# Softmax denominators of two neighbouring key tiles by one product with ones: an adaLN block with attention and experts on one core

## The chip, the core and the metric

The kernel runs on one core of a Trainium2 chip. Its engines are named as in the profile: PE (TensorE, products), DVE (VectorE), ACT (ScalarE), POOL (GpSimd) and SP (SyncE, which issues DMAs); each runs its own instructions in its own order, and semaphores order them against each other. The metric is the time of one execution on the device, in microseconds (us).

## What is computed

One transformer block over 4 batches of 2048 tokens with 256 channels, in fp32. Cut to what matters:

```python
h = layernorm(x) * (1 + ca) + sa              # per batch
q, k, v = split(h @ w_qkv)                    # 8 heads of 32
scores = q @ k.T * scale                      # causal
scores = scores + head_scales * (q[:3] . dirs) * (k[:3] . dirs)
x = x + ga * (softmax(scores) @ v) @ w_out
h = layernorm(x) * (1 + cb) + sb
shared = sum over 2 experts of gelu(h @ up) @ down
routed = the 4 most probable of 16 experts, each weighted by its probability
x = x + gb * (shared + routed)
```

What the change is about is the softmax: for each query, the exponentials of its scores are multiplied with the values, and divided by their own sum over all keys.

## The kernel before

The 8192 tokens are 16 blocks of 512 queries (`QB`); four blocks make a batch, and `qb = i % 4` is a block's place in it. A block attends to `4 * (qb + 1)` tiles of 128 keys (`kb`), for two quads `g` of four heads each. So block i has `ks = 8 * (qb + 1)` steps `(g, kb)`, numbered n, and the kernel has 320; in 224 of them all 512 queries are used, in the others (the diagonal) 384, 256 or 128.

A block has two stages. In the first (`fill_in`, called at line 1450 with steps of `project_steps`, `dense_steps`, `tile_steps` and `out_steps`) PE makes the projections of a coming block, the output projection of the block before, the shared experts and the tiles of routed experts. In the second, the summing stage (line 1456 to the end of the loop), it runs the attention of block i. The maxima of the scores of block i + 1 (`max_steps`, products `ps`, then DVE's mask and maximum) are spread over both stages.

A step of the summing stage (`sum_steps`, line 665) has three parts:

- `probabilities(kb)`, line 679: four products `st` (keys by queries, one for each head of the quad, each in a 32-row strip of PE) into two PSUM tiles of two heads each, four small products that take off the maxima, and on the diagonal four for the mask; then ACT makes two exponentials of 128x1024 (line 713) into the two halves of one SBUF tile `pt`, of which there are two (`probs`, `bufs=2`).
- `weigh(kb, 0)`, line 718: the product `av` of the probabilities with the values, added up in PSUM over all kb.
- `weigh(kb, 1)`: the product `dv` of the probabilities with `ones`, added up in another PSUM bank: the sums by which the result is divided.

The PSUM tiles of the scores come from a ring of three pairs (`mring`, line 149), which the maxima use too; the sums from `accp`, two banks. After the last kb, DVE copies the sums into `rd` (line 736), ACT copies the products into `num` (line 739), and `divide` (line 741) makes a reciprocal and a product for each of four parts, into `oT`.

The order is written out by hand. Everything of a summing stage goes into the list `part` with a key, and `run` calls it by rising key (equal keys in the order in which they were put in); each engine keeps the order in which its instructions were made (`Pinned`, line 41: hence all instructions have line 52 in the profile). Scores have key n, `av` n + 1.3, `dv` n + 1.6:

```python
        for n, (first, average, total) in enumerate(sums + more):
            part.append((n, first))
            part.append((n + 1.3, average))
            part.append((n + 1.6, total))
```

So PE's order in a step is st(n), av(n-1), dv(n-1). The products of a search for maxima have key at + 0.5, in `searched` steps (line 1486). DVE's work (divisions, the choice of experts, the two layer norms) is spread by `put` (line 1489), which books each piece with its cost in us against the `room` of a step, 2.2 us or 1.4 in a searched step, and gives it the key at + 0.6. The `ticks` (line 1524) pace POOL's gathers and scatters of routed rows at n + 0.9; the combination of gathered rows (`combine`, `complete`, line 1217, DVE's `sum`) runs with them when their rows are asked for, outside `room`. SP loads the inputs, the weights of the experts and the rows; `load_gates` has the gates of a batch made.

Of the kernel before, what the change touches and what calls it, by code (L numbers as in the profile page):

```python
# [12 lines left out]
F32 = mybir.dt.float32  # L13
# [6 lines left out]
P = 128  # L20
# [72 lines left out]
def adaln_block_kernel(  # L93
# [178 lines left out]
        for k in range(TOPK):  # L272
            nc.vector.memset(nth[:, t, k : k + 1], float(TOPK * t + k + 1))
    tile_no = const.tile([P, MAXT], F32, tag="tile_no", name="tile_no")
    tile_no_i = const.tile([P, MAXT], I32, tag="tile_no_i", name="tile_no_i")
    nc.gpsimd.iota(tile_no_i, pattern=[[1, MAXT]], base=0, channel_multiplier=0)
    nc.vector.tensor_copy(tile_no, tile_no_i)
    half_power = const.tile([P, TT], F32, tag="half_power", name="half_power")
# [139 lines left out]
    def max_steps(i, g):  # L418

        qb = i % NB  # L420
        parts = small.tile([P, TT, 4, NB], F32, tag="parts", name=f"parts{i}_{g}")
        mTs[i, g] = work.tile([P, QB], BF16, tag=f"mT{g}", name=f"mT{i}_{g}")
        steps = []

        def scores(t, ch):
            w = min(QB, (qb * TT + t + 1) * P - ch * QB)
            halves = []
            for a in range(2):
                both = pair(f"ps{i}_{g}_{t}_{ch}_{a}")
                halves.append(both)  # L430
                for u in range(2):
                    r = G * (2 * a + u)
                    nc.tensor.matmul(
                        both[:, u, :w],
                        lhsT=qTs[i][r : r + G, g, t * P : (t + 1) * P],
                        rhs=kT[r : r + G, (i - qb + ch) % SLOTS, g, :w],
                        start=True,
                        stop=True,
                        tile_position=(r, 0),
                    )  # L440
            for a, both in enumerate(halves):
                if ch == qb:
                    edge = both[:, :, w - P : w]
                    nc.vector.tensor_tensor(edge, edge, c_pair, ALU.add)
                nc.vector.tensor_reduce(
                    parts[:, t, 2 * a : 2 * a + 2, ch], both[:, :, :w], AX.X, ALU.max
                )

        def split():
            pc = pieces[g]  # L450
            ngm = small.tile([P, TT, 4], F32, tag="ngm", name=f"ngm{i}_{g}")
            nc.vector.tensor_reduce(ngm, parts[:, :, :, : qb + 1], AX.X, ALU.max, negate=True)
            for n in range(3):
                nc.vector.tensor_copy(pc[:, :, :, n], ngm)
                if n < 2:
                    nc.vector.tensor_tensor(ngm, ngm, pc[:, :, :, n], ALU.subtract)

        def turn():
            pc = pieces[g]
            pr = single([P, QB], f"pr{i}_{g}")  # L460
            for t in range(TT):
                nc.tensor.matmul(
                    pr[:, t * P : (t + 1) * P],
                    lhsT=pc[:, t].rearrange("p h n -> p (h n)"),
                    rhs=ident_b,
                    start=True,
                    stop=True,
                )
            nc.scalar.copy(mTs[i, g], pr)

        for t in range(TT):
            for ch in range(qb + 1):
                steps.append(lambda t=t, ch=ch: scores(t, ch))
        return steps, split, turn
# [183 lines left out]
        left = fill_in(merged(project_steps(2), gates_to_come[4:]), tops[:10])  # L658
        rest = tops[10:]

    probs = ctx.enter_context(tc.tile_pool(name="probs", bufs=2))
    tiles = ctx.enter_context(tc.tile_pool(name="tiles", bufs=2))
    kept = ctx.enter_context(tc.tile_pool(name="kept", bufs=3))

    def sum_steps(i, g, oT):

        qb = i % NB
        nkb = (qb + 1) * TT
        qT, mT = qTs[i], mTs[i, g]
        sums = []  # L670
        pts, held = {}, {}

        def keys(kb):
            return (i - qb + kb // TT) % SLOTS, kb % TT

        def left(kb):
            return max(0, kb - qb * TT) * P

        def probabilities(kb):
            lo = left(kb)  # L680
            slot, n = keys(kb)
            halves = [pair(f"st{i}_{g}_{kb}_{a}") for a in range(2)]
            heads = [both[:, u, :] for both in halves for u in range(2)]
            for h in range(4):
                r = G * h
                nc.tensor.matmul(
                    heads[h][:, lo:],
                    lhsT=kT[r : r + G, slot, g, n * P : (n + 1) * P],
                    rhs=qT[r : r + G, g, lo:],
                    start=True,  # L690
                    stop=False,
                    tile_position=(r, 0),
                )
            for h in range(4):
                r = G * h
                nc.tensor.matmul(
                    heads[h][:, lo:],
                    lhsT=unit3[r : r + 3, :],
                    rhs=mT[r : r + 3, lo:],
                    start=False,  # L700
                    stop=(kb < qb * TT),
                    tile_position=(r, 0),
                )
            if kb >= qb * TT:
                for h in range(4):
                    nc.tensor.matmul(
                        heads[h][:, lo : lo + P],
                        lhsT=ident_b,
                        rhs=kmask,
                        start=False,  # L710
                        stop=True,
                    )
            pt = probs.tile([P, 4, QB], F32, tag="pt", name=f"p{i}_{g}_{kb}")
            for a, both in enumerate(halves):
                nc.scalar.activation(pt[:, 2 * a : 2 * a + 2, lo:], both[:, :, lo:], AF.Exp)
            pts[kb] = pt

        def weigh(kb, s):
            if kb == 0:
                sums.append(accp.tile([P, QB], F32, tag="acc", name=f"{'ad'[s]}v{i}_{g}"))  # L720
            lo = left(kb)
            slot, n = keys(kb)
            for h in range(4):
                r = G * h
                c0 = g * P + r
                nc.tensor.matmul(
                    sums[s][r : r + G, lo:],
                    lhsT=ones if s else vA[:, slot, n, c0 : c0 + G],
                    rhs=pts[kb][:, h, lo:],
                    start=(kb == 0),  # L730
                    stop=(kb == nkb - 1),
                    tile_position=(0, r),
                )
            if kb == nkb - 1 and s:
                held["rd"] = once.tile([P, QB], F32, tag="rd", name=f"rd{i}_{g}")
                nc.vector.tensor_copy(held["rd"], sums[1])
            elif kb == nkb - 1:
                held["num"] = once.tile([P, QB], F32, tag="num", name=f"num{i}_{g}")
                nc.scalar.copy(held["num"], sums[0])

        def divide(t):
            own = slice(t * P, (t + 1) * P)
            rd = held["rd"]
            nc.vector.reciprocal(rd[:, own], rd[:, own])
            nc.vector.tensor_tensor(oT[:, g, own], held["num"][:, own], rd[:, own], ALU.mult)

        steps = [
            [
                lambda kb=kb: probabilities(kb),
                lambda kb=kb: weigh(kb, 0),  # L750
                lambda kb=kb: weigh(kb, 1),
            ]
            for kb in range(nkb)
        ]
        return steps, [lambda t=t: divide(t) for t in range(TT)]

    def out_steps(i, oT):

# [66 lines left out]
    def turn_steps(i):  # L825
# [14 lines left out]
        def logits():  # L840
            pl = single([P, TT, R], f"pl{i}")
            for t in range(TT):
                for k in range(KC):
# [4 lines left out]
                        start=(k == 0),  # L848
                        stop=(k == KC - 1),
                    )  # L850
            logs[i] = small.tile([P, TT, R], F32, tag="log", name=f"log{i}")
            nc.scalar.copy(logs[i], pl)

        return [(T_US, lambda: turn(0)), (T_US, lambda: turn(1)), (2.2, logits)]
# [1 line left out]
    def choice_steps(i, group):  # L856
# [39 lines left out]
        def chosen():  # L896
# [3 lines left out]
            held["sel"] = sel  # L900
            if group is None:

                gate = small.tile([P, TT, R], F32, bufs=1, tag="gate", name=f"gate{i}")
                parts = small.tile([P, TT, 3, R], BF16, bufs=1, tag="gate3", name=f"gate3_{i}")
                nc.vector.tensor_tensor(gate, pr[:, :, :R], sel, ALU.mult)
                for n in range(3):
# [52 lines left out]

        def weights():  # L960
            t0 = group.blocks.index(i) * TT
            wide = once.tile(shape, F32, tag="hotp", name=f"hotp{i}")
            pr = held["pr"]
            nc.vector.tensor_tensor(
                wide, hot(), pr[:, :, :R].unsqueeze(2).broadcast_to(shape), ALU.mult
# [438 lines left out]
    for i in range(NBLK):  # L1404
# [58 lines left out]
        if i == 0:  # L1463
            load_gates(0)
        oT = once.tile([P, KC, QB], F32, tag="oT", name=f"oT{i}")
        (sums, divided), (more, ends) = [sum_steps(i, g, oT) for g in range(NQ)]
        part = []
        for n, (first, average, total) in enumerate(sums + more):
            part.append((n, first))
            part.append((n + 1.3, average))  # L1470
            part.append((n + 1.6, total))
        for n, (_, ss, turn) in enumerate(rest):
            at = int(0.93 * (n + 0.5) / len(rest) * ks)
            part += [(at + 0.5, s) for s in ss]
# [45 lines left out]
        for n, j in enumerate(fresh):  # L1520
            till = 0.95 if n + 1 == len(fresh) else 0.5
            put(norm(first_norm_steps(j)), (0.15 + 0.4 * n) * ks, till * ks)

        def ticks(n):
            tick()
# [100 lines left out]
```

## Time and profile before

| | us |
|---|---|
| median of 3 runs | 2571.34 |
| the runs | 2566.7, 2571.34, 2572.5 |
| profiled execution, its own time | 2561.29 |
| profiled execution, span of the trace | 2559.6 |
| mean granted clock of TensorE in it | 0.955 of full |

| groups of the profiled execution | us busy | mean ns of one |
|---|---|---|
| PE st, 512 queries (x1792) | 324.1 | 651 |
| PE av, 512 queries (x1792) | 244.2 | 617 |
| PE dv, 512 queries (x1792) | 240.8 | 610 |
| ACT exponential 128x1024 (x448) | 434.2 | 1021 |
| DVE maximum of ps 128x1024 (x448) | 529.9 | 1221 |
| POOL gathers of rows (x224) | 216.7 | 968 |

Busy time is the time in which at least one instruction of the group ran; four strips of PE run side by side, so eight records of `dv`, one step, cover 1.075 us and not 8 x 0.61. The column "idle before" of such a group is time in which its engine had nothing to run just before an instruction of the group, and the name behind the arrow is who let it go on. A line of the timeline gives the start in us, the length, the engine, and the operation with the tiles that it writes and reads.

### The profile page before, as it was taken

Reading aid. Unit: us, or ns where it says so; the run is one execution under the profiler, and the core shown is the slowest. Engines: PE = TensorE matmul, PEld = TensorE weight load, DVE = VectorE, ACT = ScalarE, POOL = GpSimd, SP = SyncE. Lnnn points to the kernel's source line nnn. Section 1 sums busy time; section 2 is a strip of 40 time slices with the busy share of each in tenths; the row PEclk is TensorE's granted clock in tenths of the full one; section 3 lists DMA queues with packets and bytes.
Section 4 is the critical chain, followed back from the end, with each engine's and each line's share of the span. In section 5 each row is a group of like instructions: output and inputs, shape, how many; then the busy total and the mean of one; then the engine's idle time right before and its main releaser. Section 6 shows DMA issues by size and latency. Waiting matters only on the chain. (4 is left out here: it accounts for less than half of the span.)

```text
span 2559.6 us, 42608 instructions
## 1 busy us (share of the span) xinstructions
PE 2397.4 (94%) x16961; PEld 1182.3 (46%) x16961; DVE 1427.1 (56%) x2833; ACT 981.4 (38%) x1391; POOL 698.0 (27%) x740
## 2 busy tenths in 40 slices
PE   7989999999999999999999999998999998998987
PEld 4443433345544333365645344364633257335754
DVE  5577665436667774346565656458557840422235
ACT  2324244543333344534343335533342343542420
POOL 3201010421124035201013333502353320354334
PEclk9989899999999899998999999998998999999999
DMA  2300403343532112233622135233623169338943
GB/s 87 118 1 9 148 9 109 115 132 116 163 114 67 34 44 99 73 115 122 211 95 75 50 126 179 82 129 112 221 90 109 56 200 300 110 121 278 325 136 116
DMA packets 219703, 306.91 MB, mean 120 GB/s; under 512 B 18544, under 2 KB 158832, under 8 KB 219504
## 3 DMA queue, kind: packets, MB, share of 16 engines
q1 hardware_dynamic: 192720, 228.89, 27.1%
q0 software_dynamic: 25536, 73.43, 9.0%
q8 instruction: 134, 2.20, 0.4%
q10 hardware_dynamic: 1248, 1.86, 0.2%
q14 instruction: 65, 0.53, 0.1%
HBM read 193.49 MB, written 114.82 MB: 120 GB/s over the span
## 5 line engine op out<-in xcount | busy, mean ns | idle before, releaser
L52 DVE TENSOR_REDUCE parts<-ps 128x2 f32<-128x1024 f32 (+3 forms) x640 | 662.4, 1063 | 318.4 <-PE ps L52 309.3
L52 ACT ACTIVATE p<-st 128x1024 f32<-128x1024 f32 (+3 forms) x640 | 538.6, 893 | 618.8 <-PE st L52 564.4
L52 PE MATMUL st<-qT,kv 32*128 32x512 f32 (+3 forms) x2560 | 412.0, 584 | 15.2 <-ACT p L52 7.6
L52 PE MATMUL ps<-kv,qT 32*128 32x512 f32 (+3 forms) x2560 | 400.8, 614 | 22.1 <-DVE parts L52 11.9
L52 POOL DMA_INDIRECT got<-yg,at x224 | 216.7, 968 | 368.5 <-ACT p L52 96.9
L52 PE MATMUL av<-p,kv 128*32 128x512 f32 (+3 forms) x2560 | 306.6, 549 | 3.8 <-ACT p L52 2.1
L52 PE MATMUL dv<-p,ones 128*32 128x512 f32 (+3 forms) x2560 | 302.3, 541 | 1.5 <-issue 1.5
L72 POOL DMA_INDIRECT xg<-rows,at x219 | 212.8, 972 | 299.5 <-ACT p L52 121.2
L52 PEld LDWEIGHTS st<-qT,kv 32*128 32x128 f32 x2560 | 143.9, 186 | 268.9 <-issue 196.2
L52 DVE TENSOR_TENSOR ps<-ps,cmask 128x256 f32<-128x256 f32 x256 | 109.3, 427 | 253.1 <-PE ps L52 208.6
L52 PEld LDWEIGHTS ps<-kv,qT 32*128 32x128 f32 x2560 | 135.0, 194 | 229.5 <-issue 90.2
L52 POOL TENSOR_TENSOR x<-x,tmps 128x512 f32<-128x512 f32 x28 | 35.4, 1264 | 519.8 <-DVE tmps L52 519.7
L52 PE MATMUL pu<-xt,wt 128*128 128x128 f32 x1216 | 161.3, 283 | 13.9 <-DMA wt<-experts 12.2
L52 PE MATMUL py<-wt,tact 128*128 128x256 f32 x608 | 163.6, 403 | 7.6 <-ACT xt L52 2.1
L52 PEld LDWEIGHTS pu<-xt,wt 128*128 128x128 f32 x1216 | 151.4, 195 | 37.1 <-issue 12.9
L52 PE MATMUL st<-mT,unit 3*128 3x512 bf16 (+3 forms) x1280 | 165.9, 348 | 0.0
L52 PEld LDWEIGHTS dv<-p,ones 128*32 128x32 f32 x2560 | 72.4, 110 | 174.0 <-issue 168.7
L52 ACT COPY y<-py 128x512 f32<-128x512 f32 x152 | 89.0, 585 | 144.1 <-PE py L52 141.5
L52 PEld LDWEIGHTS py<-wt,tact 128*128 128x128 f32 x608 | 111.1, 196 | 50.3 <-issue 9.0
L52 DVE RECIPROCAL rd<-rd 128x128 f32<-128x128 f32 x128 | 120.8, 943 | 0.8
L52 ACT COPY xt<-px 128x512 f32<-128x512 f32 x152 | 86.3, 586 | 85.2 <-PE px L52 82.1
L52 PEld LDWEIGHTS av<-p,kv 128*32 128x32 f32 x2560 | 52.6, 108 | 137.4 <-issue 112.4
(288 smaller groups left out, 2454.0 us busy)
## 6 DMA issues: line engine op xcount, KB each, us to landing
wt<-experts SPq DMA_DIRECT2D x304, 256.0 KB
xr<-xg SPq DMA_DIRECT2D x76, 512.0 KB
yg<-y SPq DMA_DIRECT2D x76, 512.0 KB
xg<-zeros SPq DMA_DIRECT2D x16, 1024.0 KB
xin<-in_x SPq DMA_DIRECT2D x16, 512.0 KB
x<-in_x SPq DMA_DIRECT2D x16, 512.0 KB
h2d<-xnb POOLq DMA_DIRECT2D x14, 512.0 KB
pre<-x POOLq DMA_DIRECT2D x14, 512.0 KB
```

What stands on the lines that cost most here:

```text
L52: made = call(*args, **kwargs)
L72: made = call()
```

## The change

`sum_steps` gets a set `joining` and a function `join`. For a kb in `joining`, DVE adds the probabilities of kb to those of kb - 1, in place, after the exponentials of kb; the product with ones of kb - 1 is left out, and that of kb reads the added tile. A probability tile is now two tiles of two heads (halves), from four buffers; joined keys have two buffers of their own (tag "joins"). Which keys are joined is decided behind all `put`s, by what is left of `room`: kb from 1 to the first diagonal tile, kb - 1 not joined, neither step n nor n + 1 searched, and 2.2 us left in steps n - 1 and n together. The addition has key n + 1.1, the product of joined keys n + 2.55 in place of n + 1.6. To make space, `num` goes (ACT copies into `oT`, and the division is in place), and several small tiles share or lose buffers.

```diff
--- before.py
+++ after.py
@@ -272,7 +272,7 @@
         for k in range(TOPK):
             nc.vector.memset(nth[:, t, k : k + 1], float(TOPK * t + k + 1))
     tile_no = const.tile([P, MAXT], F32, tag="tile_no", name="tile_no")
-    tile_no_i = const.tile([P, MAXT], I32, tag="tile_no_i", name="tile_no_i")
+    tile_no_i = once.tile([P, MAXT], I32, tag="rows", name="tile_no_i")
     nc.gpsimd.iota(tile_no_i, pattern=[[1, MAXT]], base=0, channel_multiplier=0)
     nc.vector.tensor_copy(tile_no, tile_no_i)
     half_power = const.tile([P, TT], F32, tag="half_power", name="half_power")
@@ -418,7 +418,7 @@
     def max_steps(i, g):
 
         qb = i % NB
-        parts = small.tile([P, TT, 4, NB], F32, tag="parts", name=f"parts{i}_{g}")
+        parts = small.tile([P, TT, 4, NB], F32, bufs=2, tag="parts", name=f"parts{i}_{g}")
         mTs[i, g] = work.tile([P, QB], BF16, tag=f"mT{g}", name=f"mT{i}_{g}")
         steps = []
 
@@ -448,7 +448,7 @@
 
         def split():
             pc = pieces[g]
-            ngm = small.tile([P, TT, 4], F32, tag="ngm", name=f"ngm{i}_{g}")
+            ngm = small.tile([P, TT, 4], F32, bufs=1, tag="ngm", name=f"ngm{i}_{g}")
             nc.vector.tensor_reduce(ngm, parts[:, :, :, : qb + 1], AX.X, ALU.max, negate=True)
             for n in range(3):
                 nc.vector.tensor_copy(pc[:, :, :, n], ngm)
@@ -658,17 +658,19 @@
         left = fill_in(merged(project_steps(2), gates_to_come[4:]), tops[:10])
         rest = tops[10:]
 
-    probs = ctx.enter_context(tc.tile_pool(name="probs", bufs=2))
+    probs = ctx.enter_context(tc.tile_pool(name="probs", bufs=4))
     tiles = ctx.enter_context(tc.tile_pool(name="tiles", bufs=2))
     kept = ctx.enter_context(tc.tile_pool(name="kept", bufs=3))
 
     def sum_steps(i, g, oT):
+
 
         qb = i % NB
         nkb = (qb + 1) * TT
         qT, mT = qTs[i], mTs[i, g]
         sums = []
         pts, held = {}, {}
+        joining = set()
 
         def keys(kb):
             return (i - qb + kb // TT) % SLOTS, kb % TT
@@ -710,24 +712,32 @@
                         start=False,
                         stop=True,
                     )
-            pt = probs.tile([P, 4, QB], F32, tag="pt", name=f"p{i}_{g}_{kb}")
+            pts[kb] = []
             for a, both in enumerate(halves):
-                nc.scalar.activation(pt[:, 2 * a : 2 * a + 2, lo:], both[:, :, lo:], AF.Exp)
-            pts[kb] = pt
+                name = f"p{i}_{g}_{kb}_{a}"
+                if kb in joining:
+                    pt = probs.tile([P, 2, QB], F32, bufs=2, tag="joins", name=name)
+                else:
+                    pt = probs.tile([P, 2, QB], F32, tag="pt", name=name)
+                nc.scalar.activation(pt[:, :, lo:], both[:, :, lo:], AF.Exp)
+                pts[kb].append(pt)
 
         def weigh(kb, s):
-            if kb == 0:
+            if len(sums) == s:
                 sums.append(accp.tile([P, QB], F32, tag="acc", name=f"{'ad'[s]}v{i}_{g}"))
             lo = left(kb)
             slot, n = keys(kb)
+            if s and kb + 1 in joining:
+                return
+            of = pts[kb - 1] if s and kb in joining else pts[kb]
             for h in range(4):
                 r = G * h
                 c0 = g * P + r
                 nc.tensor.matmul(
                     sums[s][r : r + G, lo:],
                     lhsT=ones if s else vA[:, slot, n, c0 : c0 + G],
-                    rhs=pts[kb][:, h, lo:],
-                    start=(kb == 0),
+                    rhs=of[h // 2][:, h % 2, lo:],
+                    start=(of is pts[0]),
                     stop=(kb == nkb - 1),
                     tile_position=(0, r),
                 )
@@ -735,14 +745,17 @@
                 held["rd"] = once.tile([P, QB], F32, tag="rd", name=f"rd{i}_{g}")
                 nc.vector.tensor_copy(held["rd"], sums[1])
             elif kb == nkb - 1:
-                held["num"] = once.tile([P, QB], F32, tag="num", name=f"num{i}_{g}")
-                nc.scalar.copy(held["num"], sums[0])
+                nc.scalar.copy(oT[:, g, :], sums[0])
 
         def divide(t):
             own = slice(t * P, (t + 1) * P)
             rd = held["rd"]
             nc.vector.reciprocal(rd[:, own], rd[:, own])
-            nc.vector.tensor_tensor(oT[:, g, own], held["num"][:, own], rd[:, own], ALU.mult)
+            nc.vector.tensor_tensor(oT[:, g, own], oT[:, g, own], rd[:, own], ALU.mult)
+
+        def join(kb):
+            for one, other in zip(pts[kb - 1], pts[kb]):
+                nc.vector.tensor_tensor(one, one, other, ALU.add)
 
         steps = [
             [
@@ -752,7 +765,7 @@
             ]
             for kb in range(nkb)
         ]
-        return steps, [lambda t=t: divide(t) for t in range(TT)]
+        return steps, [lambda t=t: divide(t) for t in range(TT)], joining, join
 
     def out_steps(i, oT):
 
@@ -848,7 +861,7 @@
                         start=(k == 0),
                         stop=(k == KC - 1),
                     )
-            logs[i] = small.tile([P, TT, R], F32, tag="log", name=f"log{i}")
+            logs[i] = small.tile([P, TT, R], F32, bufs=2, tag="log", name=f"log{i}")
             nc.scalar.copy(logs[i], pl)
 
         return [(T_US, lambda: turn(0)), (T_US, lambda: turn(1)), (2.2, logits)]
@@ -900,7 +913,7 @@
             held["sel"] = sel
             if group is None:
 
-                gate = small.tile([P, TT, R], F32, bufs=1, tag="gate", name=f"gate{i}")
+                gate = small.tile([P, TT, R], F32, bufs=1, tag="met", name=f"gate{i}")
                 parts = small.tile([P, TT, 3, R], BF16, bufs=1, tag="gate3", name=f"gate3_{i}")
                 nc.vector.tensor_tensor(gate, pr[:, :, :R], sel, ALU.mult)
                 for n in range(3):
@@ -959,7 +972,9 @@
 
         def weights():
             t0 = group.blocks.index(i) * TT
-            wide = once.tile(shape, F32, tag="hotp", name=f"hotp{i}")
+            wide = work.tile([P, 2, C], F32, tag="tmp", name=f"hotp{i}")[:, 0, :].rearrange(
+                "p (t k e) -> p t k e", t=TT, k=TOPK
+            )
             pr = held["pr"]
             nc.vector.tensor_tensor(
                 wide, hot(), pr[:, :, :R].unsqueeze(2).broadcast_to(shape), ALU.mult
@@ -1463,12 +1478,9 @@
         if i == 0:
             load_gates(0)
         oT = once.tile([P, KC, QB], F32, tag="oT", name=f"oT{i}")
-        (sums, divided), (more, ends) = [sum_steps(i, g, oT) for g in range(NQ)]
+        quads = [sum_steps(i, g, oT) for g in range(NQ)]
+        divided, ends = [quad[1] for quad in quads]
         part = []
-        for n, (first, average, total) in enumerate(sums + more):
-            part.append((n, first))
-            part.append((n + 1.3, average))
-            part.append((n + 1.6, total))
         for n, (_, ss, turn) in enumerate(rest):
             at = int(0.93 * (n + 0.5) / len(rest) * ks)
             part += [(at + 0.5, s) for s in ss]
@@ -1520,6 +1532,23 @@
         for n, j in enumerate(fresh):
             till = 0.95 if n + 1 == len(fresh) else 0.5
             put(norm(first_norm_steps(j)), (0.15 + 0.4 * n) * ks, till * ks)
+
+
+        half = ks // NQ
+        for g, (sums, _, joining, join) in enumerate(quads):
+            for kb in range(1, qb * TT + 1):
+                n = g * half + kb
+                if kb - 1 in joining or searched & {n, n + 1}:
+                    continue
+                if room[n - 1] + room[n] >= 2.2:
+                    joining.add(kb)
+                    room[n] -= 2.1
+                    part.append((n + 1.1, partial(join, kb)))
+            for kb, (first, average, total) in enumerate(sums):
+                n = g * half + kb
+                part.append((n, first))
+                part.append((n + 1.3, average))
+                part.append((n + (2.55 if kb in joining else 1.6), total))
 
         def ticks(n):
             tick()
```

## The prediction

> **What bounds the kernel.** I read the page's busy shares, then its slices, then the groups by line and shape, then the waits of PE, and last the timeline of single steps. The shares:
>
> ```profile
> PE 2397.4 (94%) x16961; PEld 1182.3 (46%) x16961; DVE 1427.1 (56%) x2833; ACT 981.4 (38%) x1391; POOL 698.0 (27%) x740
> PE   7989999999999999999999999998999998998987
> DVE  5577665436667774346565656458557840422235
> ```
>
> PE is at 90% or more in nearly every slice, DVE at 40 to 70%. So a product that PE needn't do can be worth its slot, and DVE has time on the average. What the slot is worth is decided in the step. Groups by shape, then a plain step of block 15 (start, length, engine, operation):
>
> ```profile
> L52 PE MATMUL st<-qT,kv 32*128 32x512 f32 x1792 | 324.1, 651 | 9.5 <-ACT p L52 6.5 <-DVE parts L52 3.0
> L52 PE MATMUL dv<-p,ones 128*32 128x512 f32 x1792 | 240.8, 610 | 0.0
> ...
> L52 ACT ACTIVATE p<-st 128x1024 f32<-128x1024 f32 x448 | 434.2, 1021 | 449.1 <-PE st L52 409.4 <-issue 35.7 <-remote 3.9
> ```
>
> ```profile
> 2192.38 1.14 PE L52 MATMUL st<-qT,kv 32*128 32x512 f32 x8
> ...
> 2193.66 1.06 PE L52 MATMUL av<-p,kv 128*32 128x512 f32 x8
> ...
> 2193.82 1.94 ACT L52 ACTIVATE p<-st 128x1024 f32<-128x1024 f32 x2 [1.44 <-issue]
> ...
> 2194.55 1.04 PE L52 MATMUL dv<-p,ones 128*32 128x512 f32 x8
> ...
> 2195.52 1.14 PE L52 MATMUL st<-qT,kv 32*128 32x512 f32 x8
> ```
>
> A step is 3.14 us from st to st: av starts 1.28 after st, dv 0.88 after av, the next st 0.97 after dv. The exponentials start 1.44 after st; the first half ends at 2.46, the second at 3.38. PE waits for nothing here, with about 1 us to spare before it needs the exponentials. A second limit lies close behind. At the start of quad 1 of block 15 the diagonal steps are short and PE runs into the exponentials:
>
> ```profile
> 2238.07 1.94 ACT L52 ACTIVATE p<-st 128x1024 f32<-128x1024 f32 x2 [1.03 <-PE st L52]
> ...
> 2239.14 0.19 PEld L52 LDWEIGHTS st<-qT,kv 32*128 32x128 f32 x2 [0.18 <-ACT p L52]
> ...
> 2240.42 1.07 PE L52 MATMUL av<-p,kv 128*32 128x512 f32 x8
> ```
>
> The two score pairs of a step take two of the three in PSUM. Heads 2 and 3 of the next step (2239.14) had to wait for the first exponential of the step before (2238.07 + 1.02 = 2239.09), 0.05 before them; av came 1.28 after them. So heads 2 and 3 can't start sooner than 0.05 after the first half of the exponentials.
>
> **How many joins, and what one costs DVE.** The program of the changed kernel has 31 joins (a joined pair: keys kb-1 and kb), all over full 512 columns: 4 in block 3, 1 in 5, 6 in 7, 1 in 9, 10 in 11, 1 in 13 and 8 in 15. PE drops 31 x 4 = 124 dv matmuls, DVE gains 62 additions of 128x1024. So the change does what it says, in 31 of 224 full steps. Addition rows: sum+gbs 128x256 takes 427 ns, tmp<-po,gm 128x512 takes 689, act<-pw,act 128x1024 takes 1225 (one input in PSUM). I take 1.22 us, 2.44 a join, 76 us in all; the ends are 2 x 0.69 and 2 x 1.22 with a stretch of 0.95 on each (below). Taken alone, 31 slots of 0.88 are 27.3 us.
>
> **A join by itself.** Times from the start of st in step n, where keys n are added to keys n-1. Step n has no dv, so st(n+1) starts at 1.28 + 0.97 = 2.25; but its heads 2 and 3 wait for 2.46 + 0.05 = 2.51, 0.26 late. av(n) starts at 2.25 + 1.28 + 0.26 = 3.79. The joined product is placed a step late, so step n+1 has no dv either: st(n+2) at 4.76. Its exponential came at 2.25 + 1.44 + 0.16 (in the stall above it came 0.29 later for heads 0.47 late, and 0.26 x 0.29 / 0.47 = 0.16), its half ends at 4.87, so heads 2 and 3 are 0.16 late; av(n+1) at 6.20. Then the joined product at 7.08, the plain dv(n+1) at 7.96, st(n+3) at 8.93. Before it was 3 x 3.14 = 9.42: 0.49 us gained of the 0.88. Then the buffer: keys n+2 take the halves of keys n-1, which the joined product reads until 7.08 + 1.04 = 8.12. The exponential of n+2 starts there instead of near 6.3, its half ends at 9.14, and heads 2 and 3 of st(n+3) are 0.26 late. Freed half by half it may cost nothing. I take the middle, 0.13, and **0.36 us** for the join (0.23 to 0.49).
>
> DVE can begin at 3.38 and needs 2.44: ready at 5.82, wanted at 7.08, 1.26 to spare. Around the joins DVE's other work keeps to that, but for block 5 (below).
>
> **A join followed by another at keys n+2** (13 of the 31). There step n+2 has the joined product and no other: st(n+3) at 7.08 + 0.97 = 8.05, its heads in time. Step n+3 is short again: st(n+4) at 10.30, heads 0.26 late. From 4.76 + 0.16 to 10.56 are 5.64 against 6.28: **0.64 us** gained. The joined keys have buffers of their own, so the other wait is not there.
>
> **The 18 others**: 15 as above. Two (block 3 and 7, quad 1, key 8) have a maxima search at key 10: the joined product stands on PE behind both of the search's products, and the exponential of key 10, which wants the buffer, behind that. The search's second pair then finds no PSUM but its first's, which DVE frees after mask and maximum, 0.43 + 1.22. Followed through like the step above, 15.2 us from st(8) where the trace has 12.9 with the gain left out: about 2.5 us lost less 0.36 gained, 2.1 each. One (block 5, quad 1, key 1) meets a DVE with 6.08 of 6.40 us taken, then 3.37 of 3.47, in the two steps: its additions end some 10.5 us after st(1), wanted at 8.9; about 1.7 lost, less 0.36, is 1.3.
>
> Sum: 13 x 0.64 + 15 x 0.36 - 2 x 2.1 - 1.3 = 8.3 + 5.4 - 4.2 - 1.3 = **8.2 us** faster.
>
> **What I cost at nothing.** The copy of av into oT in place of num: the same ACT copy (590 ns), and oT was written by the division anyway; the last reader of oT, the output projection, is a block earlier. Fewer buffers of maxima and gate tiles: their writers and readers follow in order on DVE, or a block apart. The later place of the products in the order of equal keys: quad 0's sum is copied behind up to nine short DVE instructions in seven blocks, where DVE had 0.7 to 7 us idle before; at most 2 us. At the start SP's loads of two inputs pass the stores of the gates; PE's first scores, at 103.6 us, didn't wait for them. Four buffers instead of two for the dense experts' activations: the idle time that PE has there (4.3 us) is for DVE's product, not a buffer.
>
> **A lock.** DVE's additions from two inputs in SBUF meet POOL's:
>
> ```profile
> 2181.62 0.41 DVE L52 TENSOR_TENSOR sum<-sum,gbs 128x256 f32<-128x256 f32 x1
> 2181.80 1.36 POOL L52 TENSOR_TENSOR x<-x,tmp 128x512 f32<-128x512 f32 x1 [13.51 <-DVE tmp L52]
> 2182.07 1.37 DVE L52 TENSOR_TENSOR sum<-sum,row 128x256 f32<-128x256 f32 x1
> ```
>
> The second addition takes 1.37 instead of 0.43 while POOL adds: 0.95 longer. POOL's elementwise groups are 93.7 + 40.5 + 35.4 = 170 us of 2560, so some 4 of 62 additions should meet one, within 1.26 us to spare: 0 in the sum.
> The Trainium skill (SBUF — State Buffer, Who interferes with whom) says that a DVE instruction with two SBUF inputs contends with a GpSimd instruction that reads SBUF, by an exclusive lock; the trace agrees, 1.37 against 0.43, and by that rule each of the 62 additions is exposed, which speaks against the change.
>
> **Rivals.**
> (1) The slot is all that counts: the rings cost less than worked out, the exponentials move up. For it: PE's idle time by ACT in all of st is 7.6 us. Against: 2.25 is short of 2.51. 20 to 27 us faster, 2544 to 2551.
> (2) Nothing left: the gain is given back. For it: after each summing stage PE waits for weights by DMA (12.2 us in 15 places) and gathered rows (11.4), and a PE that comes sooner waits longer; or the buffer wait is 0.26 and the order costs its 2 us. 2567 to 2576.
> (3) Slower: the joined product waits on PE, in order, for a late DVE. Behind it stand the plain dv and all later scores. It decides from 1.26 us of delay. A combine (0.50 + 0.43 + 0.46) and one locked addition (0.95) ahead of a join are 2.34, 1.1 late. If 17 of 31 meet this, 17 x 1.1 = 19 us less the 8: 11 slower, 2582. For it: the room is counted per step of the program, not by when gathers land (37.8 us of DVE's idle time is for them). Against: DVE mostly idles at these steps.
>
> **How the numbers follow.** The profiled execution took 2561.29 us (span 2559.6, and 1.7 around it): 2553.1 by the sum. It is 10 us under the median of the runs, 2571.34; off the median, 2571.3 - 8.2 = **2563 us**. Forecast 0.47 (2558 to 2569; 0.34 of it faster by over 0.2%, 5.1 us, the least that a measurement of this kernel tells from no change), rival 1 0.18, rival 2 0.15, rival 3 0.20. Faster 0.52, same 0.28, slower 0.20. The range of 2547 to 2578 leaves out about half of rival 1 and half of rival 3.
>
> **What would show it.** Steps without dv of 2.4 to 2.6 us, not 2.25, with heads 2 and 3 behind ACT; the exponential of n+2 right behind the joined product where no other join follows; additions of 1.22 us; the steps of key 10 in blocks 3 and 7 over 6 us; PE busy less by some 27 us, its idle time more by some 19. Wrong if short steps run at 2.25 us, or if PE waits for joins in more than a few places.

## The result and the profile after

The changed kernel took 2556.92 us (median of 5 runs, 2552.51 to 2561.21) against 2571.21 (5 runs, 2566.7 to 2572.5): a ratio of 0.9956, 95% interval 0.9936 to 0.9976. That is 14 us faster where 8 were forecast: inside the range of 2547 to 2578, and 1 us under the forecast's own band of 2558 to 2569. The profiled execution took 2556.92 us with a span of 2555.2. That is only 4.4 us under the one of before, which was shorter than any of the timed runs of before; both have a mean granted clock of 0.955. So the two traces alone can't tell where the 14 us are; the runs below were needed for that.

The page's busy shares of the changed kernel, and its groups of dv and of the additions (line, engine, operation, count; busy us and mean ns; idle before):

```profile
PE 2384.5 (93%) x16713; PEld 1181.2 (46%) x16713; DVE 1503.9 (59%) x2895; ACT 980.1 (38%) x1391; POOL 714.9 (28%) x740
```

```profile
L52 PE MATMUL dv<-p,ones 128*32 128x512 f32 x1544 | 206.6, 610 | 1.6 <-DVE p L52 1.6
```

```profile
L52 DVE TENSOR_TENSOR p<-p,p 128x1024 f32<-128x1024 f32 x62 | 74.8, 1247 | 38.7 <-PE av L52 33.8 <-ACT p L52 4.6 <-PE st L52 0.2
```

248 records of dv are gone and 62 additions have come, 76.8 us more of DVE in all. But PE is busy only 12.9 us less (2397.4 to 2384.5): in a step without dv the scores take longer from start to end, because heads 2 and 3 wait. PE waits for an addition at dv itself once, 1.6 us.

A join by itself, block 15, quad 1, key 1, in the timeline of the changed kernel (start, length, engine, operation, idle before and who ended it; lines of other engines and weight loads left out):

```profile
2234.97 1.18 PE L52 MATMUL st<-qT,kv 32*128 32x512 f32 x6
...
2237.72 1.18 PE L52 MATMUL st<-qT,kv 32*128 32x512 f32 x8
2238.05 2.34 DVE L52 TENSOR_TENSOR p<-p,p 128x1024 f32<-128x1024 f32 x2
...
2240.05 1.33 PE L52 MATMUL st<-qT,kv 32*128 32x512 f32 x8
...
2242.40 1.90 PE L52 MATMUL dv<-p,ones 128*32 128x512 f32 x16
...
2243.48 1.94 ACT L52 ACTIVATE p<-st 128x1024 f32<-128x1024 f32 x2 [2.37 <-PE dv L52]
...
2244.23 1.45 PE L52 MATMUL st<-qT,kv 32*128 32x512 f32 x8
```

The steps from st to st are 2.75, 2.33, 4.18 and then 3.45 us, 12.7 in all, where before had 3.61 and three of 3.14, 13.03. So 0.32 us are gained, and 0.36 were forecast. The two products (2242.40, sixteen records) come together, and the exponential of key 3 starts when the joined one has ended (2243.48, released by dv): the step after it is 3.45 instead of 3.14, and here 0.3 us go back. The total hides two terms that were off in opposite directions: the second short step is 2.33 where 2.51 was forecast, and the wait for the buffer 0.31 where 0.13 was.

### The profile page after: what moved, and what is told of

It is laid out like the page before. It is cut to its first block, busy times and chain, and to the rows that moved or that the text cites. A ratio compares the mean times of both kernels' runs of the same rounds, so it can differ in the third digit from the quotient of the medians.

```text
span 2555.2 us, 42456 instructions
## 1 busy us (share of the span) xinstructions
PE 2384.5 (93%) x16713; PEld 1181.2 (46%) x16713; DVE 1503.9 (59%) x2895; ACT 980.1 (38%) x1391; POOL 714.9 (28%) x740
## 5 line engine op out<-in xcount | busy, mean ns | idle before, releaser
L52 PE MATMUL st<-qT,kv 32*128 32x512 f32 (+3 forms) x2560 | 423.6, 588 | 18.3 <-ACT p L52 11.7
L52 POOL DMA_INDIRECT got<-yg,at x224 | 222.6, 994 | 358.3 <-ACT p L52 100.1
L72 POOL DMA_INDIRECT xg<-rows,at x219 | 219.0, 1000 | 290.4 <-ACT p L52 121.3
L52 PEld LDWEIGHTS st<-qT,kv 32*128 32x128 f32 x2560 | 152.1, 186 | 282.6 <-issue 167.6
L52 PE MATMUL dv<-p,ones 128*32 128x512 f32 (+3 forms) x2312 | 267.7, 535 | 1.6 <-DVE p L52 1.6
L52 PE MATMUL st<-mT,unit 3*128 3x512 bf16 (+3 forms) x1280 | 175.0, 348 | 0.0
L52 PE MATMUL pu<-xt,wt 128*128 128x128 f32 x1216 | 157.3, 280 | 16.3 <-DMA wt<-experts 14.5
L52 PEld LDWEIGHTS dv<-p,ones 128*32 128x32 f32 x2312 | 63.5, 110 | 148.3 <-issue 137.1
L52 POOL TENSOR_TENSOR x<-x,tmp 128x512 f32<-128x512 f32 x32 | 40.5, 1267 | 278.1 <-DVE tmp L52 238.8
```

The source lines that it names most:

```text
L52: made = call(*args, **kwargs)
L72: made = call()
```

## The experiments

**The first theory** was that of the prediction: the joins move the time, everything else is worth nothing, and the short first profile of before was chance. Its rival: the other edits bring a good part. Steps below are from the start of one st to the next, (block, quad, key), in us, read from the traces. Each set of four ran on one chip beside before; the level of before moved from chip to chip (2566, 2561 and 2551 us), so ratios are compared.

The granted clock has to be read beside every time. It differs from run to run, and the time follows it: of the 23 runs of before on the first chip the longest took 2576.79 us at a mean clock of 0.949, the shortest 2554.0 at 0.958. Over the runs of all the experiments, each kernel about its own mean, 0.001 more of the clock goes with some 2.1 us less. Two kernels whose runs lie at different clocks therefore differ partly by that; "at equal clock" below is an estimate by this slope.

**Before, once more** (no edit).

> The kernel before, unchanged, with a trace of its own. Theory 1 (the joins alone move the time; the first profiled execution of before, 2561.29 us, was a short one by 5 to 10 us in stages that the change doesn't touch): 2566 to 2573 us, summing stages within 3 us in all of the first trace, the rest between summing stages longer by 3 to 10. Theory 2 (the first profile is a typical one, and the 14 us between the medians come partly from edits other than the joins): 2560 to 2564 in the profiled execution, every stage as in the first trace.

Measured: 2566.6 us, ratio 1.0000 (0.9981 to 1.0018); span 2562.9. Its stages differ from those of the first trace by up to 3.6 us, up and down: a single trace of this kernel doesn't resolve 5 us, its steps do. It decides for neither theory.

**No joins.**

```diff
-            for kb in range(1, qb * TT + 1):
+            for kb in ():
```

> The changed kernel with no key joined: halves, buffers, in-place division, order of equal keys and loads as changed, all dv products as before. Theory 1 (the joins are what moves the time): 2569 to 2573 us, as before. Theory 2 (the other edits bring half or more of the 14 us): 2558 to 2565, and the joins 1 to 7 us.

Measured: 2551.37 us, 0.9955 (0.9935 to 0.9974); the changed kernel had 0.9956 against its own runs of before. The first theory falls: a gain is there without a single join. Its size is in doubt, for the runs without joins have a mean clock of 0.957 and those of before 0.9535: of 14.5 us between the means some 7 remain at equal clock.

**Joins without the additions** (the sums lack the probabilities of the joined keys).

```diff
-                    part.append((n + 1.1, partial(join, kb)))
```

> The 31 joins without DVE's 62 additions; it leaves the keys kb of each join out of the sums. Theory 1 (joins are lost in places because DVE comes late: blocks 5 and 11, where the step of the joined product took 6.8 and 5.7 us): 6 to 10 us faster than the changed kernel, 2547 to 2551, with these steps near 4.2, and elsewhere the same steps of 2.28, 2.45, 3.20 us. Rival (DVE's additions cost nothing, all that is lost is lost in PSUM and buffers): within 2 us of the changed kernel.

Measured: 2546.73 us, 0.9935 (0.9911 to 0.9959). The steps with a late DVE get shorter: (11,0,3) from 6.79 to 3.89, (11,0,14) from 5.07 to 3.92, (11,1,14) from 4.39 to 3.37, (5,1,3) from 4.78 to 4.23; 5.6 us in all. The others stay (2.28, 2.45, 3.20). So DVE's lateness is real, in four places. In a second trace of the changed kernel (below) it is there again at two of them, (11,0,3) with 7.69 and (5,1,3) with 4.99; the two at key 14 are 3.37 there, although the additions are in it. The longest, in the first trace of the changed kernel:

```profile
1565.20 0.35 DVE L52 TENSOR_SCALAR sum<-got,weight 128x256 f32<-128x256 f32 x1 [2.72 <-DMA out<-sum]
...
1565.59 1.53 DVE L52 SCALAR_TENSOR_TENSOR sum<-got,weight,sum 128x256 f32<-128x256 f32 x3
...
1567.04 2.35 DVE L52 TENSOR_TENSOR p<-p,p 128x1024 f32<-128x1024 f32 x2
1568.31 2.19 PE L52 MATMUL dv<-p,ones 128*32 128x512 f32 x8 [1.57 <-DVE p L52]
1568.35 2.16 ACT L52 ACTIVATE p<-st 128x1024 f32<-128x1024 f32 x2 [3.38 <-DVE p L52]
```

The addition, that of key 1 to key 0, stands on DVE behind a combination of expert rows whose buffer was still being stored (2.72 us of waiting), and dv, the exponentials and the next scores wait with it. The time, 0.9935, is on the side of theory 1 against the 0.9956 of the changed kernel, but the intervals overlap: the steps decide, not the time.

**Other buffers behind a chain.**

```diff
-                if kb in joining:
+                if kb in joining or (kb - 2 in joining and kb + 1 not in joining):
```

> The keys n+2 behind a join that no other join follows take the two free buffers of the joined keys, and no longer wait for the joined product (in 16 of 18 places; in blocks 3 and 7 key 10 keeps its buffer). Theory 1 (that wait costs the step behind the joined product 0.3 to 0.4 us): the step after the one with both products goes from 3.45 to 3.14 us, 4 to 7 us faster than the changed kernel, 2550 to 2553. Rival (the wait is covered by the other exponentials): these steps stay at 3.45, time within 2 us of the changed kernel.

Measured: 2550.43 us, 0.9938 (0.9917 to 0.9960). The step behind the joined product goes from 3.45 to 3.14 at (15,1,4), from 3.78 to 3.47 at (9,0,4), from 3.79 to 3.14 at (11,0,6) and (15,0,6). The buffer wait of the prediction is real, 0.3 to 0.65 us each. Here too the time agrees with theory 1 and doesn't show it, for the intervals overlap.

**The second theory**: if not the joins, the order of equal keys. Its rivals: the halves, or the division in place.

**The order alone**, in the kernel before: the loop that lists st, av and dv moves behind all `put`s.

```diff
-        for n, (first, average, total) in enumerate(sums + more):
-            part.append((n, first))
-            part.append((n + 1.3, average))
-            part.append((n + 1.6, total))
...
+        for n, (first, average, total) in enumerate(sums + more):
+            part.append((n, first))
+            part.append((n + 1.3, average))
+            part.append((n + 1.6, total))
         def ticks(n):
```

> The kernel before with one edit: the scores and the two products of each step are put into the list after the pieces of DVE's work, so that of equal keys those pieces go first. Theory A (since the joins brought nothing, this order did: the small products of the expert choice now run ahead of the product with ones and give their PSUM pair back sooner): 0.994 to 0.997 of before, steps 7 of quad 0 in blocks 2, 6, 10 and 14 at 4.90 us in place of 5.76. Theory B (the halves of the probability tiles, freed one by one, or the other buffers): within 0.15% of before, those steps at 5.76.

Measured: 2554.68 us, 0.9966 (0.9948 to 0.9985), and the four steps at 4.90: theory A. By the medians it is 5.9 us, by the means 8.2, and at equal clock some 5 (mean clock 0.9563 against 0.9548).

**The changed kernel without joins, in the old order** (the same loop ahead of the `put`s).

> The changed kernel with no key joined, and the scores and products put into the list first, as before; it keeps the halves, the buffers and the division in place. Theory A (the order of equal keys is the gain): within 0.15% of before, steps 7 of quad 0 in blocks 2, 6, 10 and 14 at 5.76 us. Theory B (halves or buffers are the gain): 0.994 to 0.997 of before.

Measured: 2555.40 us, 0.9986 (0.9971 to 1.0000), and three of the four steps at 5.76 again, the fourth at 7.45: what is left of the gain without the order can't be told from nothing.

**The changed kernel without joins, with whole tiles**: `probs.tile([P, 4, QB])` with `bufs=2`, as before.

> The changed kernel with no key joined, and the probabilities in two whole tiles again; it keeps the new order, the other buffers and the division in place. Theory A: 0.994 to 0.997 of before, all steps as without joins. Theory B in its form with halves: within 0.15% of before.

Measured: 2547.40 us, 0.9951 (0.9937 to 0.9966). With halves it was 0.9955, on another chip: nothing shows that they are worth anything.

The steps say where the order acts: (2,0,7), (6,0,7) and (10,0,7) take 5.76 in every trace with the old order and 4.90 in every one with the new; (14,0,7) takes 7.45 or more against 4.90. These four are 0.86 x 3 + 2.55 = 5.1 us. Steps (·,0,5) of blocks 3, 5, 7, 9, 11, 13 and 15 give back 0.14 to 0.23 each, and a dozen other steps move by 0.06 to 0.44. All steps of the summing stages that differ by over 0.05 us between every trace of the old order and every one of the new without joins add up to 4.8 us for the new. That agrees with the 5 us at equal clock; what the measured 0.34% holds beyond it could not be placed. Step 7 of block 2 in before (the small products pk are those of the choice of experts):

```profile
332.46 2.36 DVE L52 TENSOR_REDUCE parts<-ps 128x2 f32<-128x1024 f32 x2 [1.18 <-PE ps L52]
...
333.40 0.18 PE L52 MATMUL pk<-selb,earlier 128*128 128x16 bf16 x1
...
333.84 1.74 PE L52 MATMUL st<-qT,kv 32*128 32x512 f32 x6
333.95 0.21 ACT L52 COPY rank<-pk 128x64 f32<-128x64 f32 x1 [1.74 <-PE pk L52]
...
334.88 0.19 PEld L52 LDWEIGHTS st<-qT,kv 32*128 32x128 f32 x2 [0.74 <-DVE parts L52]
...
336.13 1.02 ACT L52 ACTIVATE p<-st 128x1024 f32<-128x1024 f32 x1 [1.97 <-PE st L52]
```

and in the kernel with the order alone:

```profile
332.78 0.18 PE L52 MATMUL pk<-selb,earlier 128*128 128x16 bf16 x1
...
332.84 2.36 DVE L52 TENSOR_REDUCE parts<-ps 128x2 f32<-128x1024 f32 x2 [1.18 <-PE ps L52]
...
333.22 1.07 PE L52 MATMUL dv<-p,ones 128*32 128x512 f32 x8
333.33 0.21 ACT L52 COPY rank<-pk 128x64 f32<-128x64 f32 x1 [0.75 <-PE pk L52]
334.22 0.31 PEld L52 LDWEIGHTS st<-qT,kv 32*128 32x128 f32 x8 [0.84 <-DVE parts L52]
334.22 1.14 PE L52 MATMUL st<-qT,kv 32*128 32x512 f32 x8
```

Before, pk came right ahead of the scores: heads 2 and 3 took a PSUM pair of the maxima and waited for DVE until 334.82. With the new order pk runs ahead of dv, ACT has copied it out (333.33) while dv runs, and heads 2 and 3 take pk's pair: their first weight load waits for a semaphore that ACT raises, where before it was one that DVE raises. All eight records run at once. So it is at all four steps: DVE's in the traces of before, of the division in place alone and of the old order, ACT's in those of the order alone, of no joins, of whole tiles and of the changed kernel. By what rule the ring hands out another pair is not shown.

**The division in place alone**, in the kernel before.

```diff
-                held["num"] = once.tile([P, QB], F32, tag="num", name=f"num{i}_{g}")
-                nc.scalar.copy(held["num"], sums[0])
+                nc.scalar.copy(oT[:, g, :], sums[0])
```

> The kernel before with one edit: the products av are copied straight into oT and divided in place; no tile num. Theory (in before the copy for quad 1 waits until DVE has divided quad 0 out of the one num, and PE's next transposes wait for the PSUM bank behind it): PE's waits of pta for that copy go from 8.8 to 3 to 5 us, in block 1 from 3.8 to under 2; 2 to 5 us faster, 0.998 to 0.9993 of before. Rival (that wait is covered): 1.000, and the difference of the kernel with the old order has to come from buffers.

Measured: 2558.59 us against 2551.41, 1.0022 (1.0002 to 1.0042). PE's waits of pta for the copy of av do fall, from 8.8 us to 2.5, a little further than expected: with one num the copy of quad 1 had to wait until quad 0 was divided. But the time doesn't follow; if anything it is longer. Of the 5 us between the means some 3 are the clock's by the slope (0.9532 against 0.9546); the rest isn't settled.

**No joins and the changed kernel, side by side.**

> The kernel without joins again, beside the changed kernel on one chip. If the joins as placed bring nothing: the same time as the changed kernel within 3 us. If they bring the 8 us of the prediction: 6 to 10 us slower than it.

> The changed kernel again, beside the one without joins on one chip. By the steps of the two traces the 31 joins together are worth 0 to 2 us: within 3 us of it. By the prediction: 6 to 10 us faster than it.

Measured: 2527.78 us without joins, 0.9911 (0.9886 to 0.9937); 2534.54 with them, 0.9939 (0.9916 to 0.9962). In the time the 31 joins bring nothing here, and may cost up to 0.3%. But all seven runs with them have a clock of 0.956 to 0.958, and all six without 0.961 to 0.964; at equal clock the kernel with the joins would be some 6 us the faster. Nor is the lower clock a mark of joins: it is 0.958 to 0.963 with the 36 joins below, and 0.955 to 0.960 with the 25. The steps show less of it. The traces of this pair have the summing stages of blocks 3, 5, 7, 9, 11, 13 and 15 at +2.0, +0.1, +2.2, +0.2, -3.1, -0.3 and -1.9 us with joins, -0.8 in all (in the first pair of traces -2.5). So the 31 joins are worth some 1 to 6 us, by steps or by an estimate, and not the 8 forecast.

**Fewer joins, better placed.**

```diff
-                if kb in joining:
+                if kb in joining or (kb - 2 in joining and kb + 1 not in joining):
...
-                if kb - 1 in joining or searched & {n, n + 1}:
+                if kb - 1 in joining or searched & {n, n + 1, n + 2}:
+                    continue
+                if kb == qb * TT or (i, g, kb) in SKIP:
```

> The changed kernel with 25 of its joins: none where a maxima search comes two steps later, none at the first diagonal tile, none at the two places where DVE came late (block 5, quad 1, key 1 and block 11, quad 0, key 3); behind the last join of a chain the keys n+2 take the free buffers of the joined keys. From the traces: 0.63 us for a join by itself, 0.8 for one in a chain, so 10 to 14 us faster than without joins, 2537 to 2543 where that is 2551. Rival (what the steps gain is given back in the stages between, where PE waits for weights and rows): within 4 us of the kernel without joins.

Measured: 2539.51 us, 0.9924 (0.9905 to 0.9943); beside it, without joins, 0.9951 (the whole tiles): 7 us by the ratios and 8 by the medians, at nearly the same clock (0.9575 against 0.9582), under the 10 to 14 expected and over the rival's 4. The two stretches with a search, +2.3 us each in the first trace of the changed kernel, are at -1.3 (steps 6 to 14). One of the two late places was missed: what this kernel leaves out in block 11, quad 0, are the joins at keys 3 to 5, but the late addition is that of key 1, which stays, and step (11,0,3) takes 7.90 against 3.14 without joins. A joined product met in time takes a step of 4.19 ((15,1,3)), so this one place costs 3.7 us.

**More joins**: the same with `room[n - 1] + room[n] >= 1.2`.

> As the kernel with 25 joins, but 1.2 us left in two steps are enough in place of 2.2: 36 joins, 11 of them at other keys or in longer chains. If room is not what limits (0.7 us for each further join): 5 to 8 us faster than with 25, 0.989 to 0.990 of before. Rival (DVE comes late where it has less room, and PE waits in order): as with 25 or slower, 0.992 or more, with steps over 5 us at the joined products.

Measured: 2518.44 us, 0.9879 (0.9851 to 0.9906), 33 us under before and 9 under the kernel without joins on the same chip, which ran at the same clock (means 0.961 and 0.962); the best of all. So joins do pay where they are placed well, and the room asked for on DVE was not the limit. The late place is still in it: (11,0,3) takes 6.43. Its additions are a little slower, and PE's idle time at dv for them is 2.2 us in place of 1.6:

```profile
L52 DVE TENSOR_TENSOR p<-p,p 128x1024 f32<-128x1024 f32 x72 | 90.2, 1293 | 23.2 <-PE av L52 23.2
```

```profile
L52 PE MATMUL dv<-p,ones 128*32 128x512 f32 x1504 | 204.7, 606 | 2.5 <-DVE p L52 2.2
```

And part of the gain goes back in the stages between, as rival 2 of the prediction has it. The summing stages of the seven odd blocks from 3 on are 16 us shorter together than in the trace without joins from the same chip (542.3 against 558.5, each stage from its first st to its last), but PE's longest wait for gathered rows is now 15.5 us, where it is 7.7 to 9.8 in all other traces. Its waits with these joins, and with none in the first trace without joins (us in total, times, longest):

```profile
PE px L52 <- DMA xr<-xg: 20.2, 2, 15.5
```

```profile
PE px L52 <- DMA xr<-xg: 11.3, 2, 7.7
```

**All kernels at equal clock.** The differences from before on the same chip, of the means of the runs, and what is left of them at the clock of before by the slope of 2.1 us (an estimate, good to a few us: the slopes of single kernels go from 0.9 to 3.1):

| kernel | mean clock of before, of this | us from before | at equal clock |
|---|---|---|---|
| order alone | 0.9548, 0.9563 | -8.2 | -5 |
| no joins, old order | 0.9548, 0.9563 | -6.4 | -3 |
| no joins, whole tiles | 0.9548, 0.9582 | -13.0 | -6 |
| no joins, first and second set | 0.9535, 0.9572; 0.9546, 0.9620 | -14.5; -23.5 | -7; -8 |
| 31 joins (second set) | 0.9546, 0.9564 | -17.4 | -13 |
| 25 joins | 0.9548, 0.9575 | -21.6 | -16 |
| 36 joins | 0.9546, 0.9610 | -33.9 | -20 |

## Why the number was right and its cause only in part

The median fell into the range, on the side forecast. The sum behind it had two errors of opposite sign, so it is in part luck that the number came out well: of the 14 us some 5 belong to a term that was put at no gain, and 1 to 6 to the joins, which were to bring 8. What is left of the 14 is not placed; the clock of the first runs of before is not on record, and at one clock the two profiled executions are only 4.4 us apart.

- **"The later place of the products in the order of equal keys ... at most 2 us"** is the step that failed. It looked only at DVE's copy of the sums, and not at which PSUM pair the next scores get when pk is moved past dv. Alone it gains: 0.9966 (0.9948 to 0.9985), 4.8 us in the steps, 5.1 of them in four places.
- **The sum of the joins, 8.2 us**, was 0.8 and 2.5 in the summing stages of two pairs of traces, nothing in the time as measured, and some 6 at equal clock. By its terms: the join by itself held in its total (0.32 measured at (15,1,1), 0.36 forecast). The chain of four in (15,1), steps 5 to 13, went from 29.47 to 26.16 in the first pair of traces and from 28.68 to 25.86 in the second: 3.3 and 2.8 gained, 3 x 0.64 + 0.36 = 2.3 forecast. The two searches were sized too small: steps 6 to 14 of (3,1) went from 30.59 to 32.93, 2.3 lost, where -0.64 + 2.1 - 0.36 = 1.1 was forecast. And the late DVE was looked for in block 5 and not found in block 11, where the combination's wait is for a store: steps 1 to 6 of (11,0) lost 2.7 and 2.2 where 1.0 should be gained. In block 11 the joined product of key 12 falls among the short diagonal steps: steps 12 to 14 of its two quads went from 9.2 to 11.05 and 10.38 in the first trace, where DVE came late, and to 9.36 in both in the second, where it didn't. The forecast made no difference between this place and others.
- **The search at key 10** was right in its kind. In the changed kernel:

```profile
508.05 1.13 PE L52 MATMUL ps<-kv,qT 32*128 32x512 f32 x4
...
509.30 0.43 DVE L52 TENSOR_TENSOR ps<-ps,cmask 128x256 f32<-128x256 f32 x1 [2.48 <-PE ps L52]
509.76 1.23 DVE L52 TENSOR_REDUCE parts<-ps 128x2 f32<-128x1024 f32 x1
...
511.14 1.13 PE L52 MATMUL ps<-kv,qT 32*128 32x512 f32 x4 [1.96 <-DVE parts L52]
...
512.19 3.30 PE L52 MATMUL dv<-p,ones 128*32 128x512 f32 x16
...
513.80 1.94 ACT L52 ACTIVATE p<-st 128x1024 f32<-128x1024 f32 x2 [7.16 <-PE dv L52]
```

  The second pair of ps waits for DVE, the products with ones for ps, and the exponential of key 10 for them, 7.16 us after ACT's last work. The step is 9.82 in place of 4.57.
- **The ring** held in its kind: steps without dv are 2.28 and then 2.32 to 2.45 (2.25 and 2.51 forecast), so heads 2 and 3 cost less than was taken. PE's busy time fell by 12.9 and not by 27, and its idle time rose by 8.5 (162.2 to 170.7) and not by 19, since a wait inside a step's overlapping records counts as busy.
- **The lock** was rightly left out: the 62 additions take 1247 ns on average, 1.22 us was taken. The rule of the Trainium skill (SBUF — State Buffer, Who interferes with whom) shows in four of them, 1.38 to 1.75 us beside POOL's work on xnb. All that the additions took over 1.22 us is 62 x 0.027 = 1.7 us of DVE.
- **Rival 1** (the full slot) is out: no kernel here has it. **Rival 3** was right about two places in both traces and two in one, not about seventeen. **Rival 2**, nothing left of the joins, is what the times say, with the order hiding it; at equal clock a part is left. That PE gives the gain back waiting for rows or weights is seen with 36 joins and not clearly with 31 (rows 11.4 to 11.5 us, weights 12.2 to 14.5).

## What to carry to other kernels

A change that alters the order of a hand-written list is several changes: make the kernel with the order alone and the kernel with the idea alone before giving the gain to the idea. A product taken off PE is worth its slot only as far as PSUM and buffers let the next scores start, so a saving must be placed where no search, no diagonal and no DMA-bound work of DVE stands in front, and the consumer's buffer must be free: the same idea showed nothing in the time in 31 places, and 9 us in 36 places of which 20 are the same. And compare the clocks of two sets of runs before giving a difference of 0.3% to a change. Where tiles share a ring, look at which earlier tile's release the next one waits for.

## What was not expected of the hardware

PE's granted clock falls to about half for 3.4 to 20.5 us at a time, in 24 to 34 stretches of a trace, 186 to 244 us in all. Some stand at the same work in every trace (from about 52, 93, 165 and 285 us on), others come in one trace and not in another of the same kernel. In the trace of before, windows around step (2,0,1) (length, busy us of PE, PEld, DVE, ACT and POOL, granted clock, DMA share, GB/s):

```profile
301.00:304.00 3.00, 3.00 (x16) 0.91 (x16) 1.39 (x2) 0.75 (x2) 0.00 (x0) 0.55 1.03 340
304.00:308.20 4.20, 4.20 (x22) 0.84 (x24) 0.01 (x1) 1.90 (x2) 0.00 (x0) 0.51 1.04 343
308.20:314.00 5.80, 5.80 (x46) 1.57 (x48) 4.32 (x8) 2.08 (x3) 0.00 (x0) 1.00 0.39 130
```

The step took 8.12 us here, 6.78 in the second trace of the same kernel and 5.18 without joins, with the clock at 1.00. A product av then takes 1.94 us in place of 1.06. This is the noise under which 5 us have to be found: runs of one kernel on one chip spread by 20 us. Whether a change of order or the joins change how often it happens is open: the granted clock was 0.955 and 0.956 in the two traces of the changed kernel and 0.962 and 0.961 in the two without joins, but 0.963 with more joins and 0.956 without joins with whole tiles.
